# Storing results from GpSimd's queue in a two-layer convolution kernel, with rows of scales sent through DRAM

## The chip, the cores and the metric

The kernel runs on one core of one Trainium2 chip. A core has five engines that run side by side: TensorE (PE in the profile, with PEld for its weight loads), VectorE (DVE), ScalarE (ACT), GpSimd (POOL) and SyncE (SP). Any of SP, ACT and POOL can issue DMAs, and each has a queue of its own that works strictly in order: what waits at its head holds up all that stands behind it. The metric is the device time of one execution in microseconds (us), taken as the median of several runs.

## The reference

The input x is an activation of 16 images, 1024 channels, 32 x 32 pixels, in float32. Two residual blocks follow each other.

```python
# layer 0: a bottleneck with 3x3 self-attention in place of the 3x3 convolution
h = relu(bn(conv1x1(x, w_conv1)))                 # 1024 -> 256 channels
q, k = relu(bn(conv1x1(h, wq))), relu(bn(conv1x1(h, wk)))
v = bn(conv1x1(h, wv))
attn = softmax over the 9 taps of (q . (unfold3x3(k) + pos))     # 32 heads of 8 channels
h = relu(bn(sum over taps of unfold3x3(v) * attn))
x = relu(bn(conv1x1(h, w_conv3)) + x)             # 256 -> 1024 channels
# layer 1: an ordinary bottleneck
out = relu(bn(conv1x1(x, w1)))                    # 1024 -> 256
out = relu(bn(conv3x3(out, w2)))                  # 256 -> 256
x = relu(bn(conv1x1(out, w3)) + x)                # 256 -> 1024
```

The batch norm of layer 1 is built from mean, variance, gamma and beta. In the last products of both layers the scale of the norm is multiplied into the columns of the weights ahead of time; this needs the scale of each of the 1024 output channels as a row, the same in all 128 partitions.

## The kernel before

**Tiling.** Channels lie on the 128 partitions. An image has 8 chunks of 128 channels x 1024 pixels, 512 KB each. All products are float32 with 512 columns; one chunk of eight products takes PE 3.43 us. The stages of an image are written with a letter each:

- C (`first_conv`): 8 chunks of x are reduced to the 256 hidden channels (`reduce_part`, L360).
- Q and V (`project`, L446): q, k and v. They are written to DRAM and read back in another layout, by quarters of an image and heads. The reading back is called a relay here (`relay`, L534): q, k and the position terms together, and v.
- attention, on DVE alone (`logits` and `weighted`, L553 to L621): products of q with shifted k, sums over 8 channels, softmax (whose exp is L585 on ACT), and the weighted sum of shifted v. Its result a goes through DRAM back to the first layout.
- F (`fused`): for each of the 8 chunks the product of a with w3 on top of the residual, ReLU, a store of the result r to DRAM for later, and at once the reduction of that chunk with u1 for layer 1. The hidden result goes to `vh`, and DVE transforms it (`transform`, L668 to L679) for a Winograd form of the 3x3 convolution.
- W (`winograd_conv`, L737): the 3x3 convolution of four images together.
- U (`last_sum`): for each of the 8 chunks the product with u3 on top of the residual r, ReLU, and the store of the output.

**Expanding products.** F and U share the class `Expand`. `seed` (L384, ACT) copies a residual chunk, loaded from DRAM, into PSUM, two chunks ahead; `products` (L391, PE) adds to it; `result` applies ReLU with the bias (L410, ACT), in place in the chunk that held the residual, and issues the store of it (L411), on ACT's queue.

**Chunk buffers.** `xpool` has 8 buffers for chunks. `more_loads` issues the next loads in a fixed list (x for C, s for F, r for U, and the transformed V for W) whenever `credits` says that a buffer is free; the load (L336) goes out on POOL's queue, except for the first image's eight chunks of x, which go out on ACT's. In F and U `free(True)` gives a buffer back one chunk late, because the chunk's store has to land before the buffer is loaded again. Relays also go out on POOL's queue; weights, halves of attention's traffic and the scaled weights on SP's.

**Order.** The order of work on each engine is fixed when the program is built. The stages follow four lines of text; `Side` simulates DVE beside PE and decides between which chunks attention, transforms and weight preparation stand. Nothing is reordered on the chip.

**Semaphores of DMAs.** DMAs of SP and ACT take turns on eight completion semaphores, those of POOL on eight others. An issue waits until the DMA that had its semaphore before has landed.

**The start.** `at_first` loads eight chunks of x, then the taps of the 3x3 convolution (`load_taps`: six loads of 384 KB on ACT), then w3 and u3 for scaling (`load_scaled`: four of 512 KB on ACT), and four pieces of weights on SP. `winograd_weights` (L275 to L283, DVE and ACT) turns the taps into 36 Winograd weight planes. `scale_rows` (L225 to L238) makes the two rows of 1024 scales: DVE spreads the scales on diagonals (L229), PE multiplies them with a matrix of ones (L236), and ACT copies the result from PSUM (L238). `scale_weights` (L245) multiplies w3 and u3 with the rows on DVE.

Of the kernel before, what the change touches and what calls it, by code (L numbers as in the profile page):

```python
# [8 lines left out]
F32 = mybir.dt.float32  # L9
AF = mybir.ActivationFunctionType  # L10
ALU = mybir.AluOpType
AX = mybir.AxisListType

P = 128
B, C, H, W = 16, 1024, 32, 32
HW = H * W
WID = 256
NC = C // P
# [3 lines left out]
KK = 9  # L22
HEAD_DIM = 8
EPS = 1e-5
RELU = AF.Relu
CHUNKS = 8
NJ = 4
JROWS = H // NJ
JPIX = JROWS * W
PW = W + 2  # L30
HALO = (JROWS + 2) * PW
# [40 lines left out]
def sa_bottleneck_kernel(ctx: ExitStack, tc: tile.TileContext, x, w1t, wqkvt, w3t, u1t, u2t, u3t, params, out):  # L72
    nc = tc.nc
# [3 lines left out]
    const = ctx.enter_context(tc.tile_pool(name="const", bufs=1))  # L77
# [3 lines left out]
    apool = ctx.enter_context(tc.tile_pool(name="apool", bufs=1))  # L81
    ppool = ctx.enter_context(tc.tile_pool(name="ppool", bufs=2))
    zpool = ctx.enter_context(tc.tile_pool(name="zpool", bufs=3))
    psum = ctx.enter_context(tc.tile_pool(name="psum", bufs=4, space=bass.MemoryType.PSUM))
    dram = ctx.enter_context(tc.tile_pool(name="dram", bufs=1, space=bass.MemoryType.DRAM))
# [52 lines left out]
    def col(name, j, n=1):  # L138
        return par[:, _COL[name] + j : _COL[name] + j + n]
# [25 lines left out]
    for base, sign in ((0, 1), (HEAD_DIM - 1, -1)):  # L165
        nc.gpsimd.affine_select(
            out=members,
            in_=members,
            compare_op=ALU.is_ge,
            fill=0.0,  # L170
            base=base,
            pattern=[[-sign * HEAD_DIM, G]],
            channel_multiplier=sign,
# [7 lines left out]
    for n in range(NW):  # L181
# [12 lines left out]
        )  # L194


    ones = const.tile([P, P], F32, tag="ones", name="ones")
    nc.gpsimd.memset(ones, 1.0)
    eye = const.tile([P, P], F32, tag="eye", name="eye")
    nc.gpsimd.affine_select(  # L200
        out=eye, in_=ones, compare_op=ALU.is_equal, fill=0.0, base=0, pattern=[[-1, P]], channel_multiplier=1
    )

    kp = const.tile([P, NW, H + 2, PW], F32, tag="kp", name="kp")
    nc.gpsimd.memset(kp, 0.0)
    vh = const.tile([P, NW * VROWS, VW], F32, tag="vh", name="vh")

    scaled, scales = {}, []  # L210

# [12 lines left out]
    def scale_rows():  # L224

        for which, scale in enumerate((col("L0_conv_bn3_s", 0, NC), bn_inv[:, 2 * NW : 2 * NW + NC])):
            row = psum.tile([P, C], F32, tag="ps", name="row")
            diag = zpool.tile([P, HW], F32, tag="z", name="diag")
            nc.vector.tensor_tensor(  # L229
                diag.rearrange("p (o m) -> p o m", m=P),  # L230
                eye.unsqueeze(1).to_broadcast([P, NC, P]),
                scale.unsqueeze(2).to_broadcast([P, NC, P]),
                ALU.mult,
            )
            for half in range(2):
                nc.tensor.matmul(row[:, halves(half)], ones, diag[:, halves(half)], start=True, stop=True)  # L236
            scales.append(zpool.tile([P, HW], F32, tag="z", name="scales"))
            nc.scalar.activation(scales[which], row, AF.Identity)  # L238

    def scale_weights():  # L240

# [10 lines left out]

    taps = []

    def load_taps():
        n = 3 * WID

        for m, (tag, shape) in enumerate((("e", [P, KK, JPIX]), ("bnv", [P, HEAD_DIM, HALO]))):
            t = apool.tile(shape, F32, tag=tag, name="g").rearrange("p a b -> p (a b)")
            g = [t[:, i * n : (i + 1) * n] for i in range(3)]  # L260
            for i in range(3):
                nc.scalar.dma_start(g[i], u2t[m * P : (m + 1) * P, i * n : (i + 1) * n])
            taps.append(g)

    def winograd_weights():

# [46 lines left out]
    def halves(half):  # L313
        return slice(half * HALF, (half + 1) * HALF)


    loads, loaded, stored, credits, freed = [], {}, {}, [CHUNKS], []

    def more_loads():

        while credits[0] and loads:
            kind, b, c = loads[0]
            if kind == "V":
                if forms.get(b, 0) < NK:
                    return
                src = form_room(b)[c[0], c[1]].rearrange("p k j e -> p (k j e)")
            elif kind == "r":
                if (b, c) not in stored:
                    return
                src = stored[b, c]  # L330
            else:
                src = x[b, c * P : (c + 1) * P, :]
            t = xpool.tile([P, NK * 2 * PART], F32, tag="x", name=f"{kind}_{b}_{c}".translate(str.maketrans(" ,", "__", "()")))
            t = t if kind == "V" else t[:, :HW]

            (nc.scalar if kind == "x" and b == 0 else nc.gpsimd).dma_start(t, src)  # L336
            loaded[loads.pop(0)] = t
            credits[0] -= 1
# [34 lines left out]
    class Expand:  # L373
# [28 lines left out]
        def result(self, o, to):  # L402
            t = self.tiles.pop(o)
            ps, to_ = self.ahead.pop(o), t

            if self.kind == "s":
                ps, to_ = ps.rearrange("p (n j) -> p j n", j=4), t.rearrange("p (j n) -> p j n", j=4)
            else:
                ps, to_ = ps.rearrange("p (j n) -> p n j", j=4), t.rearrange("p (n j) -> p n j", j=4)
            nc.scalar.activation(to_, ps, RELU, bias=self.shift(o), scale=1.0)  # L410
            nc.scalar.dma_start(to, t)  # L411
            return t

    sums = {}
# [242 lines left out]
    def form_room(b):  # L657
        b -= b % NK
        if b not in form_rooms:
            form_rooms[b] = dram.tile([NI, 3, P, NK, 2, PART], F32, tag=f"v{b}", name="v")  # L660
        return form_rooms[b]
# [269 lines left out]
    for text in (  # L931
        "P0 P1 P2 P3 F0 P4 F1 P5 P6 F2 P7 F3 C8 Q8 W0 V8 C9 U0 Q9 V9 U1 U2 U3",
        "F4 F5 P10 F6 F7 C11 Q11 W4 V11 C12 U4 Q12 V12 U5 U6 U7",
        "F8 F9 P13 F10 F11 C14 Q14 W8 V14 C15 U8 Q15 V15 U9",
        "F12 F13 F14 U10:0123 F15 U10:4567 U11:0123 W12 U11:4567 U12 U13 U14 U15",
    ):
        for word in text.split():
            b, _, of = word[1:].partition(":")
            for letter in "CQV" if word[0] == "P" else word[0]:
                kind = {"C": "conv1", "Q": "qk", "V": "v", "F": "fused", "W": "wino", "U": "u3"}[letter]  # L940
                stages.append((kind, int(b), [int(o) for o in of] or range(NC)))
# [185 lines left out]
    made = []  # L1127

    def at_first():
        more_loads()  # L1130
        load_taps()
        load_scaled()
        for _ in range(4):
            more_weights()
        side.first(winograd_weights(), 24.0, 0.0)
        side.first(scale_weights(), 24.0, 0.0)
        scale_rows()
        hooks["conv1", 2, 0] = clear_hidden

    at_first()  # L1140
    for at in range(len(stages)):
        run(at)
# [40 lines left out]
```

## Time and profile before

| | before |
|---|---|
| time, median of 3 runs | 2469.91 us (2467.1 to 2471.02) |
| span of the profiled execution | 2473.1 us |
| PE busy | 2403.9 us, 97% |
| DVE busy | 2079.4 us, 84% |
| ACT busy | 933.5 us, 38% |
| POOL busy | 276.0 us, 11% |
| HBM traffic | 286 GB/s over the span |
| stores of r and of the output | 128 + 128, 512 KB each |
| loads of x, s and r from POOL | 120 + 128 + 128, 512 KB each |

The page gives the busy time of each engine, the chain of work that ended last, the costliest groups of instructions and the DMA issues. In a name such as `ps<-a,w` the tile written stands ahead of the arrow and the tiles read behind it. A name such as ACTq or SPq means the engine's sequencer, which issues DMAs; such an issue isn't counted as busy. The list of waits says for whom an engine stood idle: total, times, longest. A timeline line gives start, length, engine, line of the kernel, operation, tiles and, in brackets, the idle time before it and what ended it. L numbers are lines of the kernel before.

### The profile page before, as it was taken

The numbers are of one execution on the slowest core, as the hardware profiler recorded it, in microseconds if no ns is written. First come the engines' busy times: TensorE is split into PE (matmuls) and PEld (weight loads), VectorE is DVE, ScalarE is ACT, GpSimd is POOL, SyncE is SP. The second block draws the span as 40 slices with busy tenths as digits, with TensorE's granted clock in tenths as the row PEclk, the third lists the DMA queues.
The fourth block names the chain that finished last, engine by engine and source line by source line (L and its number), as shares of the span: only waits on it lengthen the run. The fifth ranks groups of instructions, "written<-read, shape, count | busy, mean of one in ns | idle before, by whom it ended". The sixth has DMA issues, their size and how long they took to land.

```text
span 2473.1 us, 18299 instructions
## 1 busy us (share of the span) xinstructions
PE 2403.9 (97%) x6152; PEld 1158.0 (47%) x6152; DVE 2079.4 (84%) x1633; ACT 933.5 (38%) x875; POOL 276.0 (11%) x523
## 2 busy tenths in 40 slices
PE   8999999999999999999989998999999989989999
PEld 3444444443475444444475443444466434434844
DVE  5899999998989999999789988899989989964700
ACT  4324142324123574243113573334122453344276
POOL 1110100010011111001011011001011010000111
PEclk9999999999999999999999999999999999989999
DMA  9969696978597998796598997688798887788887
GB/s 359 354 235 306 233 299 205 308 252 278 198 349 261 328 361 317 247 301 253 192 367 275 301 356 272 242 293 293 239 355 275 280 321 259 272 289 283 316 285 259
DMA packets 326060, 708.88 MB, mean 287 GB/s; under 512 B 20560, under 2 KB 199760, under 8 KB 317264
## 3 DMA queue, kind: packets, MB, share of 16 engines
q0 software_dynamic: 73728, 307.00, 35.5%
q1 hardware_dynamic: 203424, 249.39, 31.3%
q10 hardware_dynamic: 48816, 151.33, 15.7%
q8 instruction: 49, 0.80, 0.1%
q14 instruction: 43, 0.35, 0.0%
HBM read 432.62 MB, written 275.02 MB: 286 GB/s over the span
## 4 chain that ended last, share of the span: by engine, by line
PE 77%; DVE 10%; DMA 9%; ACT 2%; issue 1%; SPq 0%; ACTq 0%; DVEq 0%
PE ps L360 31%; PE ps L391 25%; PE ps L446 11%; PE ps L737 8%; DVE acc L604 3%; DVE acc L617 3%; DMA a<-a 2%; DMA U<-uw 2%; DMA q<-q 1%; DMA bnk<-kp 1%; DMA a<-acc 1%; DVE form L668 1%; PE ps L484 1%; DVE v L668 1%; DMA u<-in_u1t_dram 1%
## 5 line engine op out<-in xcount | busy, mean ns | idle before, releaser
L391 PE MATMUL ps<-a,w 128*128 128x512 f32 x1024 | 465.2, 600 | 14.6 <-ACT a L643 9.4
L360 PE MATMUL ps<-s,u 128*128 128x512 f32 x1024 | 462.8, 597 | 12.6 <-ACT s L410 12.5
L391 PE MATMUL ps<-y,u 128*128 128x512 f32 x1024 | 442.0, 593 | 1.9 <-ACT ps L384 1.9
L360 PE MATMUL ps<-x,w 128*128 128x512 f32 x1024 | 442.1, 592 | 0.0
L553 DVE TENSOR_TENSOR prod<-qc,bnk 128x2048 f32<-128x2048 f32 x144 | 324.0, 2287 | 14.3 <-DMA a<-acc 12.6
L604 DVE TENSOR_TENSOR acc<-e,bnv 128x2048 f32<-128x2048 f32 x144 | 327.5, 2283 | 3.6
L391 PEld LDWEIGHTS ps<-a,w 128*128 128x128 f32 x1024 | 196.6, 193 | 266.0 <-issue 227.4
L360 PEld LDWEIGHTS ps<-s,u 128*128 128x128 f32 x1024 | 195.5, 191 | 261.3 <-issue 235.2
L391 PEld LDWEIGHTS ps<-y,u 128*128 128x128 f32 x1024 | 194.2, 190 | 247.9 <-issue 226.6
L360 PEld LDWEIGHTS ps<-x,w 128*128 128x128 f32 x1024 | 194.6, 190 | 244.9 <-issue 244.2
L410 ACT ACTIVATE s<-ps,par 128x1024 f32<-128x1024 f32 x128 | 142.5, 1113 | 416.7 <-PE ps L391 414.9
L617 DVE TENSOR_TENSOR acc<-acc 128x2048 f32<-128x2048 f32 x128 | 293.4, 2292 | 4.4
L446 PE MATMUL ps<-h,wqk 128*128 128x512 f32 x512 | 225.8, 595 | 5.7 <-ACT h L989 5.7
L410 ACT ACTIVATE r<-ps,bn_sh 128x1024 f32<-128x1024 f32 x128 | 141.8, 1108 | 80.4 <-PE ps L391 78.4
L558 DVE TENSOR_TENSOR prod<-prod 128x2048 f32<-128x2048 f32 (+1 forms) x80 | 166.2, 2077 | 2.3
L446 PEld LDWEIGHTS ps<-h,wqk 128*128 128x128 f32 x512 | 96.2, 190 | 132.7 <-issue 110.0
L384 ACT ACTIVATE ps<-s 128x1024 f32<-128x1024 f32 x128 | 131.3, 1026 | 66.0 <-ACT s L410 42.3
L384 ACT ACTIVATE ps<-r 128x1024 f32<-128x1024 f32 x128 | 130.9, 1024 | 62.3 <-ACT r L410 34.9
L989 ACT ACTIVATE h<-ps,par 128x1024 f32<-128x1024 f32 x32 | 38.5, 1205 | 282.8 <-PE ps L360 282.8
L336 POOL DMA_DIRECT2D s<-in_x_dram x128 | 67.8, 529 | 647.0 <-PE ps L360 357.3
L336 POOL DMA_DIRECT2D x<-in_x_dram x120 | 63.6, 531 | 630.8 <-PE ps L360 387.7
L458 ACT ACTIVATE kp<-ps,par 128x1024 f32<-128x1024 f32 x64 | 77.3, 1208 | 141.8 <-PE ps L446 120.4
(312 smaller groups left out, 2125.4 us busy)
## 6 DMA issues: line engine op xcount, KB each, us to landing
s<-in_x_dram POOLq DMA_DIRECT2D x128, 512.0 KB, 6.3
r<-s ACTq DMA_DIRECT2D x128, 512.0 KB, 4.4
r<-r POOLq DMA_DIRECT2D x128, 512.0 KB, 6.0
out_dram<-r ACTq DMA_DIRECT2D x128, 512.0 KB, 5.5
x<-in_x_dram POOLq DMA_DIRECT2D x120, 512.0 KB, 4.4
v<-v SPq DMA_DIRECT2D x96, 408.0 KB, 5.4
U<-uw SPq DMA_DIRECT2D x72, 512.0 KB, 7.6
bnk<-kp SPq DMA_DIRECT2D x32, 680.0 KB, 8.4
```

Of the source, the lines that this page charges most:

```text
L336: (nc.scalar if kind == "x" and b == 0 else nc.gpsimd).dma_start(t, src)
L360: nc.tensor.matmul(ps[n][:, halves(half)], wt[:, c % (NC // 2), n * P : (n + 1) * P], src[:, halves(half)], start=(c == 0), stop=(c == NC ...
L384: nc.scalar.activation(ps, t, AF.Identity)
L391: nc.tensor.matmul(self.ahead[o][:, halves(half)], pieces[key][:, n, o % (NC // 2) * P :][:, :P], self.src[:, n, halves(half)], start=Fals ...
L410: nc.scalar.activation(to_, ps, RELU, bias=self.shift(o), scale=1.0)
L446: nc.tensor.matmul(ps[:, halves(half)], pieces[key][:, m, at : at + P], h[:, m, halves(half)], start=(m == 0), stop=(m == NW - 1),)
L458: nc.scalar.activation(dst, src, func, bias=col(f"L0_conv_{name}_b", n), scale=col(f"L0_conv_{name}_s", n),)
L553: nc.vector.tensor_tensor(by_row(t[:, two]), by_row(qc), kc[:, :, i : i + JROWS, j : j + W], ALU.mult)
L558: nc.vector.tensor_add(u[:, :, 0:4], u[:, :, 0:4], u[:, :, 4:8])
L604: nc.vector.tensor_tensor(by_row(dst), rows(e[:, k, :]).unsqueeze(1).to_broadcast([P, HEAD_DIM, JROWS, W]), vc[:, :, i : i + JROWS, j : j ...
L617: nc.vector.tensor_add(acc, acc, t)
L737: nc.tensor.matmul(acc[i][:, at, :, n, :], pieces[key][:, m, at, n * P : (n + 1) * P], v[:, at, :, m * (TILES + TR) :][:, :, :TILES], star ...
```

## The change

Four edits, in one step:

- **Stores.** `result` issues the store of a finished chunk on POOL's queue instead of ACT's. ACT then only computes there; POOL's queue holds loads, relays and stores in one order.
- **Rows of scales.** `scale_rows` no longer uses DVE, PE and ACT. The scales, which lie one per partition and chunk, are written to DRAM as one row of 1024 (in pieces of 4 bytes), and the row is read back into all 128 partitions. Both go on SP's queue. The matrix of ones and the identity are no longer made.
- **Taps.** The first image's loads are issued as four chunks of x, half of the taps, three chunks, the other half, the last chunk, so that the taps come earlier.
- **Order of U11.** The chunks of U11 are split 5 and 3 around W12 instead of 4 and 4, which shifts one chunk ahead of the Winograd stage.

```diff
--- before.py
+++ after.py
@@ -194,18 +194,11 @@
         )
 
 
-    ones = const.tile([P, P], F32, tag="ones", name="ones")
-    nc.gpsimd.memset(ones, 1.0)
-    eye = const.tile([P, P], F32, tag="eye", name="eye")
-    nc.gpsimd.affine_select(
-        out=eye, in_=ones, compare_op=ALU.is_equal, fill=0.0, base=0, pattern=[[-1, P]], channel_multiplier=1
-    )
-
-
 
     kp = const.tile([P, NW, H + 2, PW], F32, tag="kp", name="kp")
     nc.gpsimd.memset(kp, 0.0)
     vh = const.tile([P, NW * VROWS, VW], F32, tag="vh", name="vh")
+
 
     scaled, scales = {}, []
 
@@ -224,18 +217,11 @@
     def scale_rows():
 
         for which, scale in enumerate((col("L0_conv_bn3_s", 0, NC), bn_inv[:, 2 * NW : 2 * NW + NC])):
-            row = psum.tile([P, C], F32, tag="ps", name="row")
-            diag = zpool.tile([P, HW], F32, tag="z", name="diag")
-            nc.vector.tensor_tensor(
-                diag.rearrange("p (o m) -> p o m", m=P),
-                eye.unsqueeze(1).to_broadcast([P, NC, P]),
-                scale.unsqueeze(2).to_broadcast([P, NC, P]),
-                ALU.mult,
-            )
-            for half in range(2):
-                nc.tensor.matmul(row[:, halves(half)], ones, diag[:, halves(half)], start=True, stop=True)
-            scales.append(zpool.tile([P, HW], F32, tag="z", name="scales"))
-            nc.scalar.activation(scales[which], row, AF.Identity)
+            row = dram.tile([NC, P], F32, tag=f"row{which}", name="row")
+            nc.sync.dma_start(row.rearrange("o p -> p o"), scale)
+            t = zpool.tile([P, HW], F32, tag="z", name="scales")
+            nc.sync.dma_start(t, AP(row.tensor, row.offset, [[0, P], [1, C]]))
+            scales.append(t)
 
     def scale_weights():
 
@@ -252,15 +238,15 @@
 
     taps = []
 
-    def load_taps():
+    def load_taps(m):
         n = 3 * WID
 
-        for m, (tag, shape) in enumerate((("e", [P, KK, JPIX]), ("bnv", [P, HEAD_DIM, HALO]))):
-            t = apool.tile(shape, F32, tag=tag, name="g").rearrange("p a b -> p (a b)")
-            g = [t[:, i * n : (i + 1) * n] for i in range(3)]
-            for i in range(3):
-                nc.scalar.dma_start(g[i], u2t[m * P : (m + 1) * P, i * n : (i + 1) * n])
-            taps.append(g)
+        tag, shape = (("e", [P, KK, JPIX]), ("bnv", [P, HEAD_DIM, HALO]))[m]
+        t = apool.tile(shape, F32, tag=tag, name="g").rearrange("p a b -> p (a b)")
+        g = [t[:, i * n : (i + 1) * n] for i in range(3)]
+        for i in range(3):
+            nc.scalar.dma_start(g[i], u2t[m * P : (m + 1) * P, i * n : (i + 1) * n])
+        taps.append(g)
 
     def winograd_weights():
 
@@ -408,7 +394,7 @@
             else:
                 ps, to_ = ps.rearrange("p (j n) -> p n j", j=4), t.rearrange("p (n j) -> p n j", j=4)
             nc.scalar.activation(to_, ps, RELU, bias=self.shift(o), scale=1.0)
-            nc.scalar.dma_start(to, t)
+            nc.gpsimd.dma_start(to, t)
             return t
 
     sums = {}
@@ -932,7 +918,7 @@
         "P0 P1 P2 P3 F0 P4 F1 P5 P6 F2 P7 F3 C8 Q8 W0 V8 C9 U0 Q9 V9 U1 U2 U3",
         "F4 F5 P10 F6 F7 C11 Q11 W4 V11 C12 U4 Q12 V12 U5 U6 U7",
         "F8 F9 P13 F10 F11 C14 Q14 W8 V14 C15 U8 Q15 V15 U9",
-        "F12 F13 F14 U10:0123 F15 U10:4567 U11:0123 W12 U11:4567 U12 U13 U14 U15",
+        "F12 F13 F14 U10:0123 F15 U10:4567 U11:01234 W12 U11:567 U12 U13 U14 U15",
     ):
         for word in text.split():
             b, _, of = word[1:].partition(":")
@@ -1127,8 +1113,14 @@
     made = []
 
     def at_first():
+        credits[0] = 4
         more_loads()
-        load_taps()
+        load_taps(0)
+        credits[0] = 3
+        more_loads()
+        load_taps(1)
+        credits[0] = CHUNKS - 7
+        more_loads()
         load_scaled()
         for _ in range(4):
             more_weights()
```

## The prediction

> **What bounds the kernel now.** I read the page's busy shares and chain first, then what TensorE (PE) waited for, then the chain and ScalarE's (ACT's) timeline around its longest avoidable wait, last the DMA by stretch.
>
> ```profile
> PE 2403.9 (97%) x6152; PEld 1158.0 (47%) x6152; DVE 2079.4 (84%) x1633; ACT 933.5 (38%) x875; POOL 276.0 (11%) x523
> ...
> PE 77%; DVE 10%; DMA 9%; ACT 2%; issue 1%; SPq 0%; ACTq 0%; DVEq 0%
> ```
>
> PE works 2404 of 2473 us, so all that any change of queues can win is 69 us. VectorE (DVE) at 84% runs close beside it. Who held PE up:
>
> ```profile
> PE ps L360 <- ACT s L410: 12.5, 4, 7.7
> PE ps L737 <- issue: 10.5, 2, 8.0
> PE ps L391 <- ACT a L643: 9.4, 2, 4.8
> PE row L236 <- DVE diag L229: 8.0, 1, 8.0
> PE ps L391 <- ACT ps L384: 7.1, 5, 5.0
> ```
>
> Columns: total us, times, longest. The L410 and L384 rows (ReLU and seed) are ACT being late, the L643 row is image 15's attention arriving late, L236 is the start. The longest, 7.7 us at 1504.83, in ACT's timeline:
>
> ```profile
> 1492.02 1.11 ACT L410 ACTIVATE s<-ps,par 128x1024 f32<-128x1024 f32 x1 [2.32 <-PE ps L391]
> 1502.33 0.33 ACTq L411 DMA_DIRECT2D r<-s  x1
> 1502.71 1.03 ACT L384 ACTIVATE ps<-s 128x1024 f32<-128x1024 f32 x1 [9.58 <-DMA u<-in_u1t_dram]
> ```
>
> The ReLU ends at 1493.13, its store is issued only at 1502.33, and ACT stands still for 9.2 us. The chain there says for what:
>
> ```profile
> 1487.22 15.04 DMA u<-in_u1t_dram
> 1502.26 0.02 issue
> 1502.28 0.02 ACTq L411
> ```
>
> A store of s has no use for weights u. In the built program SP's and ACT's DMAs take turns on eight completion semaphores, and an issue waits until the semaphore's last DMA has landed. Five ACT stores wait over 1.6 us so: 5.9 before 940.51, 9.2 before 1502.33, 4.9 before 1977.60, 4.4 before 1999.35, 1.7 before 2100.14. PE shows two: 7.7 us at 1504.83, and 1.1 at 1983.85 with 5.0 at 2002.83.
>
> Last, the transfers: the issue lines (KB, us to landing), and two stretches of result chunks (columns: length; busy us of PE, PEld, DVE, ACT, POOL; clock; DMA share; GB/s):
>
> ```profile
> r<-s ACTq DMA_DIRECT2D x128, 512.0 KB, 4.4
> r<-r POOLq DMA_DIRECT2D x128, 512.0 KB, 6.0
> out_dram<-r ACTq DMA_DIRECT2D x128, 512.0 KB, 5.5
> ...
> 838.00:932.00 94.00, 93.84 (x219) 41.33 (x218) 89.06 (x53) 65.78 (x62) 14.16 (x27) 1.00 1.00 361
> ...
> 2344.00:2473.00 129.00, 124.16 (x291) 54.87 (x289) 10.22 (x16) 83.27 (x78) 15.35 (x29) 1.00 0.78 266
> ```
>
> The stages of u3 are where DMA is tight: one load and one store of 512 KB per 3.43 us, beside attention's traffic. Pairing each load's landing with the seed reading it, the residual is ready 0 to 6 us ahead in 858-925, 0 to 9 in 1420-1480 and 4 to 9 in the last 100 us, against 12 us or more in the stages of w3.
>
> **What the Trainium skill says.** "DMA: Bandwidth & Descriptors", section "Anatomy of one DMA": DMA engines do not wait on semaphores; the issuing sequencer waits before dispatch. The trace agrees: ACT's 9.2 us. Same page, "Issuing engines are not separate DMA queues": queues share 16 engines, so another queue saves only issue time (ACT's 0.33 us against GpSimd's (POOL's) 0.53 here). Section "Queues, rings and completion order": engines go round the queues packet by packet, each queue in order; so a store moved to POOL's queue lands behind the loads and relays issued before it. No view of before shows that case. "TensorE: Matmul & The Clock Gate", "What's actually happening": PE starts at half clock for about 3.4 us of work; here the first ones (L236) stood 0.86 us apart up to 12.45, then 0.43.
>
> **Part by part.**
>
> *Stores on POOL, ACT's side.* 256 issues of 0.33 us leave ACT (85 us, mostly beside idle time: ACT is 38% busy), and with them the semaphore waits. PE's stall at 1504.83 goes: 7.7 us plus about 0.7 at half clock after it, 8.4. At 1979-2003 5.0 + 1.1 and some 1.3 around them: 7. Do they reach the end? DVE waits for ACT's exp 16.5 us before 1552.26 (2.2 is the exp itself), for PE 7.0 before 1825.65, and 11.1 before 2001.89; so DVE moves up with PE. PE's waits for image 15's attention (4.8 at 2184, 4.6 at 2191) follow from DVE, so they move too. Upper bound 15.4; lower 8 if DVE keeps only the first. I take 15.
>
> *Stores on POOL, the queue's side.* POOL pays 256 x 0.53 = 136 us of issue on top of 276: not a bound. The cost is order. Built, the queue in a u3 stage runs: store k, load into the buffer of k-1, store k+1, load into that of k. The load waits for store k-1 to land, and store k+1 stands behind it. With landing time L two chunks then take at least L + 2 x 0.53 us; PE takes 6.87, so L up to 5.8 is free. In the last stretch stores land in 3.2 to 5 us: free. In 849-932 they took 4.3 to 7.7, mostly 6.5 to 7: 7 gives 8.1, or 0.6 us per chunk. Six images' u3, 48 chunks, lie in 838-932 and 1403-1490: none to 30 us, before slack of 3 to 6 us in each stretch. Fewer stores in flight also land sooner, which argues for the low part. Add the relays: q, k and positions (2.9 MB) go out on POOL at 787, 890, 1445; in 1448-1451 even ACT's stores took 9 us, and stores behind the relay may take 4 more. And the load of r at 829.04 now comes after a store issued at 849.94 while its seed starts at 852.80: about 3 us. Part of this hides: PE waits 8.0 us for DVE's transforms at 1249.33 anyway. I take 8 lost, from 0 to 30.
>
> In w3 stages the loads come some 4.1 us later (after the next ReLU, not just the last product), hidden by 12 us of slack. Relays are delayed by up to 30 us (579.30 to behind a store of 608.86), but q lands 87 us before its use at 675.6; the other delayed q and k relays, by up to 10 us, have 30 us or more. Nothing.
>
> *Rows of scales.* Off: DVE 2 x 1.22, PE 5.91, ACT 1.94 us. On, all on SP: twice a 4 KB store in 4-byte pieces, then a 512 KB load that waits for it. No row shows 4-byte data; a row store is at least the 2.3 us of the quickest load at the start (w, issued 0.81, landed 3.14) and, I estimate, at most the 8.7 of an x load behind a full queue; I take 4. The scales are first read at 80.58 (L245), so they are hidden themselves. But ACT's loads now take semaphores in turn with them: x7's issue waits for the second scales. That chain is x0's landing at 10.9 (its semaphore), row 4, then wv's landing at 18.0 (another), scales 8.7, so x7 goes out at 27 and lands at 32 (5 us). PE can begin when x0 has landed, 10.88, and now pays the half clock itself (some 2.2 us): as good as a start at 13.1 against 13.77, and x7 is due at 13.1 + 7 x 3.43 = 37.1. Hidden with 5 us to spare. Gain 0.7, from -3 (rows at 8.7 each) to 2.
>
> *Taps between chunks.* DVE waits 18.1 us for them before 27.23. The first three may land at 19 now. But ACT, which makes the second operand (L273, at 27.47 before), must first issue x7 and the w3/u3 loads behind it, at 27-28. No gain, from -2 to 2.
>
> *U11 split 5:3.* W12 starts 2.5 us late for the transforms' V and waits 1.9 for U; a chunk of 3.43 us moved ahead of W12 fills that. The stored buffer it holds delays V loads that have 6 us or more (landed 2296.7, used 2303.0). Gain 3, from 0 to 3.4.
>
> *End.* The last store is issued 0.2 us later and may land 0.3 later: -0.5.
>
> Sum: 15 + 0.7 + 0 + 3 - 8 - 0.5 = 10.2 us. 2469.9 - 10.2 = **2460**.
>
> **Rivals.** (1) *The whole gain stays*: with fewer DMAs taking SP's semaphores in turn and fewer stores in flight, nothing is lost in u3: 2469.9 - 18.2 = 2452. For it: PE was full at DMA 100% in 838-932. Against: 0 to 6 us of slack there. (2) *Eaten up*: the queue costs 18 instead of 8, and does it where DVE waits for ACT's exp (885.27 by 1.2 us, 1440.54 by 4.9), so that DVE slips as well: 2470. For it: those waits. Against: PE's 8.0 us to spare at 1249. (3) *Slower*: POOL's queue is the bound of u3 stages: 30 us of throttle and 12 of relays (4 each) against 12 of slack and 18 of gain: 2470 + 12 = 2482. For it: POOL's loads of r already wait 249 us for out stores. Against: landing time falls when fewer are in flight.
>
> **Numbers.** Forecast 0.48, rival 1 0.19, rival 2 0.13, rival 3 0.20. The low end, 2444, is rival 1 with DVE's waits for transfers before it (12.6 us at 1198.57, 5.2 at 411.53) shortened by 8 too. The high end, 2484, is rival 3 with the start 2 us worse. Faster by over 0.2% (under 2465): 0.66; within: 0.14; slower: 0.20.
>
> **What would show it.** Right: ACT has no idle time ended by a DMA that isn't its own data, and PE no 7.7 us at 1504; PE's first product comes at about 11 us; in u3 stages POOL's stores wait behind loads, and seeds (L384) wait for loads of r by some us near 852 and 1450; the gap before W12 is under 2 us. Wrong: seeds wait in the last 100 us, where landing time must stay under 5.8; PE waits for x7 in the first 40 us; DVE's waits for exp don't shrink with PE's stalls, so that the 15 us stay with PE; or relays reach DVE late.

## The result and the profile after

The changed kernel takes 2476.94 us (median of 4 runs, 2476.71 to 2478.05), the kernel before in the same session 2469.61 us. The ratio is 1.0032, with a 95% interval of 1.0014 to 1.0049: slower by 0.3%, where the prediction said 2460. A second measurement on another chip gave 1.0029 (1.0019 to 1.0040). The experiments below ran on chips on which the kernel before takes 2462 to 2465 us, so they are compared by ratio; 0.001 is about 2.5 us. A ratio is worked out over all runs and can differ by some 0.001 from the quotient of two medians. The profiled runs lie closer together than the medians: the one of before took 2475.2 us, the one of the changed kernel 2476.75.

First the busy times and the chain on the page of the changed kernel (L numbers are now its own: the seed L384 is L370, the products L391 are L377, the ReLU L410 is L396, the store L411 is L397, the products of C and of r with u1, L360, are L346; later, the lines of an experiment have the numbers of its own kernel).

```profile
PE 2399.6 (97%) x6144; PEld 1153.9 (47%) x6144; DVE 2076.7 (84%) x1631; ACT 919.0 (37%) x873; POOL 411.0 (17%) x777
...
PE 76%; DMA 12%; issue 5%; DVE 3%; ACT 1%; POOL 1%; ACTq 0%; SPq 0%; POOLq 0%; DVEq 0%
```

PE works as long as before; POOL has its 135 us of store issues, as predicted. The chain has changed hands: DMA was 9% and is 12%, and DVE fell from 10% to 3%. Next, the list of what PE waited for (total us, times, longest):

```profile
PE ps L346 <- DMA x<-in_x_dram: 24.1, 5, 9.3
PE ps L377 <- ACT ps L370: 12.1, 9, 3.6
PE ps L432 <- ACT h L975: 9.0, 13, 3.7
PE ps L723 <- issue: 6.3, 1, 6.3
...
PE ps L346 <- ACT s L396: 1.0, 1, 1.0
```

The last row answers to the 12.5 us of `ACT s L410` at the head of the list before: the waits of ACT's stores are gone, as predicted. The first row is new, 24.1 us for chunks of x. All of it lies in the first 54 us: 9.3 until PE's first product at 9.26 (before, the diagonals had 8.0 in that place), and 14.8 between the chunks after it. The wait for seeds grew from 7.1 to 12.1.

Where does the 24.1 come from? The chain of the first 80 us, cut to the pieces with the two rows (start, length, what):

```profile
5.57 14.10 DMA row<-par
19.68 0.34 SPq L223
...
20.12 21.22 DMA row<-bn_inv
41.36 0.35 ACTq L248
```

Two stores of 4 KB take 14.1 and 21.2 us from issue to landing. Part of that is SP's queue: the first stands behind the load of wv, which lands at 15.57, the second behind the first load of scales, which lands at 29.25. From there on they take 4.1 and 12.1 us more. A tap load on ACT goes out in the very moment in which the second row has landed, though it needs nothing of it: in the built program it has the next turn on that store's semaphore. x7 waits in the same way for the second load of scales: issued at 47.38 and landed at 53.42, against a forecast of 27 and 32. Image 0's hidden result comes from ACT at 61.7 us instead of 39.7. What it waits for last is the taps: PE is done with x7's products at 59.2, but ACT, which works in order, is still at the taps, the first of which it could begin only at 49.84.

Busy times by stretch say what else was slow. First the kernel before, then the changed one (length; busy us of PE, PEld, DVE, ACT, POOL; granted clock; DMA share; GB/s):

```profile
6.00:20.00 14.00, 11.98 (x23) 5.30 (x24) 2.96 (x8) 0.00 (x0) 0.69 (x1) 1.00 1.01 379
20.00:42.00 22.00, 22.00 (x52) 9.50 (x50) 13.02 (x25) 10.13 (x19) 3.48 (x7) 1.00 1.04 397
```

```profile
6.00:20.00 14.00, 10.74 (x21) 4.82 (x22) 0.37 (x4) 0.00 (x0) 1.21 (x2) 1.00 0.89 210
20.00:42.00 22.00, 14.39 (x28) 5.71 (x27) 0.96 (x1) 0.00 (x0) 1.58 (x3) 0.84 0.93 266
```

The DMA engines are still busy 89 and 93% of the time, but they move 210 and 266 GB/s instead of 379 and 397. The page counts 22672 packets under 512 bytes where it counted 20560: the 2112 more are mostly the 2048 pieces of 4 bytes. The trace's records of single packets show that the pieces themselves are short, 0.01 us each. It is the packets of the other transfers that become long. Those of 2 KB and more (mostly 4 KB) take 0.15 to 0.16 us on average from 26 to 32 us; from 12 to 20 us, while the first row is written, they take 0.31 to 0.95, and from 32 to 38 us, while the second is, 0.26 to 1.21.

Later the lost 22 us come back, though not steadily. The changed kernel is behind by 23.0 us at the first fused stage (240.1 against 217.1 us), 17.5 at the first Winograd stage, 27.0 at F6 (1114.5 against 1087.5), 14.7 at F9, 2.3 at F13, and 0.5 at PE's end. That is the stores' gain, less what they cost. What they cost is seen in GpSimd's timeline, behind a relay (start, length, operation, and in brackets the idle time before it and what ended it):

```profile
916.66 0.53 POOL L520 DMA_DIRECT2D qc<-q  x1
...
918.22 0.54 POOL L397 DMA_DIRECT2D out_dram<-r  x1
920.22 0.53 POOL L322 DMA_DIRECT2D r<-r  x1 [1.46 <-DMA out_dram<-r]
920.74 0.54 POOL L397 DMA_DIRECT2D out_dram<-r  x1
930.97 0.53 POOL L322 DMA_DIRECT2D r<-r  x1 [9.69 <-DMA out_dram<-r]
...
937.53 0.53 POOL L322 DMA_DIRECT2D r<-r  x1 [3.01 <-DMA out_dram<-r]
```

The store issued at 918.22 lands only behind the relays of 916.66 to 917.70, and at the head of the queue the next load but one waits 9.7 us for it, with every later store and load behind. ACT's seed, at 932.03, has waited 8.2 us for its chunk of r. From then on load and store go in lockstep: each load waits until the last store but one before it has landed, and the next store stands behind that load. This takes 3.5 to 4.2 us per chunk where PE takes 3.43. The same happens behind the relay of 1466.72. The issue lines (KB, us to landing) show it as longer landings, 5.1 for r and 6.5 for the output, against 4.4 and 5.5 on ACT's queue:

```profile
r<-s POOLq DMA_DIRECT2D x128, 512.0 KB, 5.1
r<-r POOLq DMA_DIRECT2D x128, 512.0 KB, 5.8
out_dram<-r POOLq DMA_DIRECT2D x128, 512.0 KB, 6.5
```

And at W12 the loads of the transformed V stand behind the output stores of U11:

```profile
2274.86 0.53 POOL L397 DMA_DIRECT2D out_dram<-r  x1 [2.95 <-ACT r L396]
2275.55 0.53 POOL L322 DMA_DIRECT2D V__0_8020<-v  x1 [0.16 <-issue]
```

The first v's that it needs had landed by 2270.52. The load goes out 5 us later, after the fourth store of U11, lands at 2283.03, and PE stands 6.3 us, against 2.5 before.

### The profile page after: what moved, and what is told of

Its sections match the earlier page's. It is cut to its first block, busy times and chain, and to the rows that moved or that the text cites. A ratio compares the mean times of both kernels' runs of the same rounds, so it can differ in the third digit from the quotient of the medians.

```text
span 2474.9 us, 18390 instructions
## 1 busy us (share of the span) xinstructions
PE 2399.6 (97%) x6144; PEld 1153.9 (47%) x6144; DVE 2076.7 (84%) x1631; ACT 919.0 (37%) x873; POOL 411.0 (17%) x777
## 2 busy tenths in 40 slices
DMA packets 328429, 709.94 MB, mean 287 GB/s; under 512 B 22672, under 2 KB 201872, under 8 KB 319632
## 4 chain that ended last, share of the span: by engine, by line
PE 76%; DMA 12%; issue 5%; DVE 3%; ACT 1%; POOL 1%; ACTq 0%; SPq 0%; POOLq 0%; DVEq 0%
PE ps L346 33%; PE ps L377 23%; PE ps L432 12%; DMA out_dram<-r 7%; PE ps L723 7%; DMA q<-q 1%; PE ps L470 1%; DMA row<-bn_inv 1%; POOL r L322 1%; DVE acc L590 1%; DMA U<-uw 1%; DVE acc L603 1%; ACT h L975 1%; DMA s<-in_x_dram 1%; DMA row<-par 1%
## 5 line engine op out<-in xcount | busy, mean ns | idle before, releaser
L377 PE MATMUL ps<-a,w 128*128 128x512 f32 x1024 | 463.2, 597 | 10.0 <-ACT ps L370 5.2
L346 PE MATMUL ps<-x,w 128*128 128x512 f32 x1024 | 449.5, 599 | 24.1 <-DMA x<-in_x_dram 24.1
L346 PE MATMUL ps<-s,u 128*128 128x512 f32 x1024 | 458.2, 592 | 1.0 <-ACT s L396 1.0
L377 PE MATMUL ps<-y,u 128*128 128x512 f32 x1024 | 444.9, 595 | 7.1 <-ACT ps L370 6.9
L346 PEld LDWEIGHTS ps<-x,w 128*128 128x128 f32 x1024 | 196.7, 193 | 273.7 <-issue 251.1
L377 PEld LDWEIGHTS ps<-a,w 128*128 128x128 f32 x1024 | 194.9, 191 | 260.7 <-issue 239.6
L396 ACT ACTIVATE s<-ps,par 128x1024 f32<-128x1024 f32 x128 | 142.5, 1113 | 463.3 <-PE ps L377 390.7
L377 PEld LDWEIGHTS ps<-y,u 128*128 128x128 f32 x1024 | 194.4, 191 | 255.7 <-issue 236.9
L346 PEld LDWEIGHTS ps<-s,u 128*128 128x128 f32 x1024 | 194.3, 190 | 246.7 <-issue 237.5
L397 POOL DMA_DIRECT2D r<-s x128 | 68.2, 533 | 732.4 <-ACT s L396 715.7
L396 ACT ACTIVATE r<-ps,bn_sh 128x1024 f32<-128x1024 f32 x128 | 141.8, 1109 | 105.6 <-PE ps L377 100.7
L370 ACT ACTIVATE ps<-r 128x1024 f32<-128x1024 f32 x128 | 130.4, 1021 | 58.5 <-DMA r<-r 45.5
L370 ACT ACTIVATE ps<-s 128x1024 f32<-128x1024 f32 x128 | 131.1, 1024 | 22.5 <-DMA s<-in_x_dram 18.8
L746 ACT ACTIVATE z<-ps 128x1024 f32<-128x1024 f32 x48 | 49.0, 1024 | 183.4 <-PE ps L723 127.8
```

What stands on the lines that cost most here:

```text
L346: nc.tensor.matmul(ps[n][:, halves(half)], wt[:, c % (NC // 2), n * P : (n + 1) * P], src[:, halves(half)], start=(c == 0), stop=(c == NC ...
L370: nc.scalar.activation(ps, t, AF.Identity)
L377: nc.tensor.matmul(self.ahead[o][:, halves(half)], pieces[key][:, n, o % (NC // 2) * P :][:, :P], self.src[:, n, halves(half)], start=Fals ...
L397: nc.gpsimd.dma_start(to, t)
```

## The experiments

Theory after the result: the way of the scales through DRAM lost the 22 us, and the stores would have won. The rival: delays at the start are soaked up by later waits anyway, and the stores on GpSimd's queue lose.

| run | what it has | us | before | ratio, 95% interval |
|---|---|---|---|---|
| e1_rows_back | changed, rows on TensorE again | 2453.37 | 2465.13 | 0.9954 (0.9938 to 0.9970) |
| e2_only_rows | before + rows through DRAM | 2495.25 | 2465.13 | 1.0110 (1.0093 to 1.0128) |
| e3_only_stores | before + all stores on GpSimd | 2453.39 | 2465.13 | 0.9948 (0.9936 to 0.9960) |
| e4_only_taps | before + taps between chunks | 2466.85 | 2465.13 | 1.0009 (0.9998 to 1.0019) |
| e5_after_again | the changed kernel | 2470.65 | 2462.39 | 1.0029 (1.0019 to 1.0040) |
| e6_rows32 | changed, rows in 32-byte pieces | 2455.23 | 2462.39 | 0.9967 (0.9956 to 0.9978) |
| e7_rows32_hold2 | e6 + loads held back one store | 2445.44 | 2462.39 | 0.9925 (0.9911 to 0.9938) |
| e8_rows_on_pool | changed, row stores on GpSimd | 2464.50 | 2462.39 | 1.0012 (1.0002 to 1.0023) |
| e9_rows_back_hold2 | e1 + loads held back one store | 2436.82 | 2463.43 | 0.9888 (0.9866 to 0.9911) |
| e10_stores_u11 | e3 + split of U11 | 2448.65 | 2463.43 | 0.9937 (0.9914 to 0.9959) |
| e11_out_on_pool | before + output stores on GpSimd | 2468.41 | 2463.43 | 1.0020 (1.0008 to 1.0031) |
| e12_r_on_pool | before + stores of r on GpSimd | 2435.16 | 2463.43 | 0.9885 (0.9865 to 0.9905) |
| e13_only_u11 | before + split of U11 | 2462.31 | 2462.39 | 1.0002 (0.9991 to 1.0012) |
| e14_r_on_pool_u11 | e12 + split of U11 | 2434.44 | 2462.39 | 0.9891 (0.9876 to 0.9907) |

**The parts one by one.** In e1 the rows are made as before, and the rest of the change stays:

```diff
-            row = dram.tile([NC, P], F32, tag=f"row{which}", name="row")
-            nc.sync.dma_start(row.rearrange("o p -> p o"), scale)
-            t = zpool.tile([P, HW], F32, tag="z", name="scales")
-            nc.sync.dma_start(t, AP(row.tensor, row.offset, [[0, P], [1, C]]))
-            scales.append(t)
+            row = psum.tile([P, C], F32, tag="ps", name="row")
...
+            for half in range(2):
+                nc.tensor.matmul(row[:, halves(half)], ones, diag[:, halves(half)], start=True, stop=True)
+            scales.append(zpool.tile([P, HW], F32, tag="z", name="scales"))
+            nc.scalar.activation(scales[which], row, AF.Identity)
```

> The changed kernel with one part undone: the rows of scales are made on TensorE and ScalarE again; stores on GpSimd's queue, taps between the first chunks and the new split of U11 stay. Theory A (the way through DRAM lost the time: its two row stores of 14.1 and 21.2 us put the start 22 us behind, and nothing later gave that back): first products and h 0 at the times of the kernel before (within 3 us), and the whole some 20 us under the changed kernel, 2455 to 2459 us. Rival B (the delay of the start is soaked up by later waits on VectorE, and the stores on GpSimd's queue are what loses): the start comes back but the end moves by under 7 us, 2470 to 2476 us.

Measured: 0.9954. Image 0's hidden result is 0.4 us behind the first profile of before, and against the changed kernel (1.0032) the ratio is 0.9923, some 19 us. Theory A holds.

e2 is the kernel before with the lines marked minus above put in.

> The kernel before with one part alone: the rows of scales through DRAM. Theory A: row stores of 14 and 21 us again, stalls of TensorE near 32 and 53 us, +18 to +24 us at the end: 2488 to 2494 us. Rival B (soaked up later): under +8, 2470 to 2478 us. Rival C (the slow row needs the company of the taps and more loads around it, which this kernel does not have in that place): row stores under 10 us and +0 to +5 us.

Measured: 1.0110, 27 us, more than any theory said; the profiled run was the quickest, 20 us above the median of before. The rows alone take 14.1 and 24.7 us, and here the taps stand behind x7 in ACT's queue, so that image 0's hidden result comes at 65.4. Rival C fell: the rows are as slow without the early taps beside them.

e3 is the kernel before with one word changed:

```diff
-            nc.scalar.dma_start(to, t)
+            nc.gpsimd.dma_start(to, t)
```

> The kernel before with one part alone: results are stored by GpSimd's queue. Theory A (the stalls at 598, 1249, 1504 and 1977 to 2003 us go, some 8, 7, 8 and 6 us, and loads behind waiting stores lose 6 us each in the two u3 stages of r and 3 us in W0): 2456 to 2460 us. Rival B (what the lockstep of stores and loads takes equals what ScalarE wins): 2467 to 2472 us.

Measured: 0.9948, a gain of 12.8 us, near the upper end of what theory A gave. The rival of a net zero fell.

e4 has the new `load_taps(m)` and the order of `credits` of the diff, and nothing else.

> The kernel before with one part alone: the taps are loaded between the first chunks, with the credits of the changed kernel. Theory A: no row store slows the transfers, so nothing waits for the taps: 2467 to 2472 us. Rival: the order of loads itself puts chunk 7 behind the taps, a stall of 2 to 6 us of TensorE before 60 us that stays to the end: 2472 to 2476 us.

Measured: 1.0009, no difference that the interval shows. Chunk 7 comes in time: image 0's hidden result is at 39.4.

**What in the rows cost it: the size of the pieces or the turns?** e5 is the base for the next three.

> The changed kernel once more, as the base on this chip for the three kernels beside it. Every theory: slower than the kernel before by 0.2 to 0.6%, row stores of about 14 and 21 us again, first h of TensorE's chunks some 22 us behind.

The time came as expected. The rows took 16.1 and 14.3 us here, and the hidden result came at 58.1, 18 us late and not 22. e6 keeps queue, order and waits, and changes the pieces:

```diff
-            row = dram.tile([NC, P], F32, tag=f"row{which}", name="row")
-            nc.sync.dma_start(row.rearrange("o p -> p o"), scale)
+            row = dram.tile([P, NC], F32, tag=f"row{which}", name="row")
+            nc.sync.dma_start(row, scale)
...
-            scales.append(t)
+            scales.append(t.rearrange("q (p o) -> q o p", o=NC))
```

> The changed kernel, with the rows of scales stored in the order in which a partition holds them, 128 pieces of 32 bytes in place of 1024 of 4 bytes, and read back as before; VectorE reads the scales through a view with a step of 8 elements. The queues, waits and the order of issue stay. Theory A (the 4-byte pieces cost the time): row stores of 2 to 5 us each, no stall of TensorE over 3 us before 60 us, h 0 within 4 us of the kernel before, and the whole 0.3 to 0.7% under the kernel before. Rival B (the turns cost it: transfers of ScalarE's queue that wait for the scales issued on SyncE's, whatever the size of their pieces): the first x of image 0 and the taps still wait for the scales, h 0 stays 10 us or more behind, and the whole is within 0.3% of the kernel before. Rival C: the strided read slows VectorE's products by 2 us and more each, and h 0 or the first attention is late for that.

The chain at its start:

```profile
5.56 10.31 DMA row<-par
...
16.33 5.67 DMA row<-bn_inv
```

The whole gains 16 us over the changed kernel (0.9967 against 1.0029 to 1.0032), as theory A has it. Its row stores are longer than the 2 to 5 us that it gave, but by SP's queue alone: wv lands at 15.66 and the first row 0.2 us later, the first scales at 21.64 and the second row 0.4 us later. Of the 35 us in the changed kernel, then, some 19 are this queue and 16 (4.1 and 12.1) the small pieces. x7 goes out at 29.2 us, where the prediction's chain had 27. That the two are so near is in part luck: the chain had left out what stands ahead of the rows in SP's queue. The hidden result comes at 43.5, 4 us behind e4's; the turns cost no more than that here. Rival C is true in small: the four products with the view's step of 8 take 2.02 to 2.04 us each (L233) instead of 1.22 (L245 before), 3.2 us of DVE in all.

e8 leaves the pieces in the program and takes away the turns behind them: the same two 4-byte stores on GpSimd's queue, read back there in the stage of image 1.

```diff
-            nc.sync.dma_start(row.rearrange("o p -> p o"), scale)
+            nc.gpsimd.dma_start(row.rearrange("o p -> p o"), scale)
```

> The changed kernel with the same two 4-byte row stores at the same place of the program, but on GpSimd's queue, and the scales read back on that queue only in the stage of image 1. No transfer of ScalarE's or SyncE's then has to take its turn behind them. Theory A1 (the small pieces hold up whatever moves beside them): the transfers from 6 to 42 us still run at 60 to 75% of the kernel before, h 0 is 8 to 20 us behind, and the whole is 5 us and more above the kernel with rows of 32 bytes. Theory A2 (small pieces are only slow themselves, and the turns made the others wait for them): the throughput of the first 42 us stays within 10% of the kernel before, h 0 under 5 us behind, and the whole is within 4 us of the kernel with rows of 32 bytes.

Transfers and PE at its start (GB/s in 40 slices of the first 40 us; then PE's first work):

```profile
GB/s 0 28 274 214 291 76 306 331 345 96 97 101 99 121 96 97 96 254 351 168 126 355 412 412 406 414 401 417 393 426 411 394 415 402 405 410 401 405 395 395
```

```profile
15.51 30.36 PE L352 MATMUL ps<-x,w 128*128 128x512 f32 x64 [15.51 <-DMA x<-in_x_dram]
```

For 8 us, from 9 to 17, while both rows are under way (they land at 15.5 and 19.3), everything together moves 96 to 121 GB/s; from 22 us on it is some 400. PE's first chunk arrives at 15.5 us instead of 9.3. So small pieces hold up what moves beside them, as theory A1 says, also where nothing has its turn behind them. Its figures were too large: from 6 to 42 us 79% of the kernel before's transfers are moved, and the hidden result is 6.4 us behind, between the two theories. The whole, 1.0012, does not measure the start alone: reading the scales at 90 us made DVE wait 13.5 us for them (L237), which is this kernel's own fault. Nor is e8 the changed kernel without its turns: its page counts only 96 packets under 512 bytes more than before's, so that on GpSimd's queue the pieces don't show as packets of their own.

How the 22 us of the start divide between the turns and the slowed transfers stays open. In the two stretches above (379 to 210 GB/s over 14 us, 397 to 266 over 22 us) transfers worth 6.2 + 7.3 = 13.5 us were not moved. Some of them were slowed, as the long packets show, and some were not yet issued; these runs don't tell how many.

**What in the stores cost and won.** e7 adds one thing to e6: in `free(True)`, two buffers in place of one are held back.

```diff
-            credits[0] += len(freed) - 1
-            del freed[1:]
+            credits[0] += max(0, len(freed) - 2)
+            del freed[2:]
```

> The kernel with rows in pieces of 32 bytes, with one thing more: in the u3 stages a load is released only with the second store before it, so that GpSimd's queue does not stand at a load that waits for the store just issued. Theory A (loads and stores in lockstep on one queue cost 4 to 7 us at each of the two places near 930 and 1480 us): the gaps of GpSimd behind its relays stay, but the lockstep after them goes, and the whole is 4 to 12 us under the kernel without it. Rival B (the stores behind the relay are late anyway, and one buffer less in flight costs what the lockstep did): within 3 us of it, or slower.

Measured: 0.9925 against 0.9967, 10 us. PE's waits for seeds, first in e6, then in e7:

```profile
PE ps L377 <- ACT ps L370: 12.1, 6, 4.7
```

```profile
PE ps L377 <- ACT ps L370: 1.3, 2, 1.0
```

With the edit the output stores also land sooner, in 4.9 us instead of 6.5. The lockstep is real. e9 has this edit on top of e1.

> The two things that the runs so far point to, together: the changed kernel with the rows of scales made on TensorE again, and with loads in the u3 stages released only by the second store before them. Theory A (the start and the lockstep are separate losses, and their cures add): the ratio of the first, 0.9954, and what the held-back buffer gave in pieces of 32 bytes, 0.9925 / 0.9967 = 0.9958, give 0.991, so 2440 to 2445 us where the kernel before takes 2463 to 2465. Rival B (the later start of the kernel with 32-byte rows was soaked up, so that its cure gives nothing): 0.9925 again.

Measured: 0.9888, 16 us under e1 and 27 us under the kernel before: somewhat more than expected, though the interval just reaches theory A's 0.991. In its timeline of GpSimd the head of the queue still waits behind the relay, but shorter, and the chunks behind it catch up at 2.5 to 3.2 us each, under PE's 3.43:

```profile
899.44 0.53 POOL L338 DMA_DIRECT2D r<-r  x1 [5.05 <-DMA out_dram<-r]
...
904.43 0.53 POOL L338 DMA_DIRECT2D r<-r  x1 [1.29 <-DMA out_dram<-r]
```

e11 and e12 part the two kinds of stores: the output's alone (`self.kind == "r"`), and those of r alone (`"s"`).

```diff
-            nc.scalar.dma_start(to, t)
+            (nc.gpsimd if self.kind == "r" else nc.scalar).dma_start(to, t)
```

> The kernel before, with the stores of the last results alone (stage u3, the output) moved to GpSimd's queue; stores of r stay on ScalarE's. Theory A (the gain of ScalarE's side lies in both kinds of stage, the lockstep of loads and stores comes where loads of r wait for stores): about half of the gain of all stores, TensorE's stalls at 1977 to 2003 us gone, those at 598 and 1504 us still there, 0.996 to 0.9985. Rival B (these stores are the ones that cost on GpSimd's queue, since loads share it): 1.000 or above, and the kernel that moves the other kind takes 0.993 or less.

> The kernel before, with the stores of r alone (the fused stages) moved to GpSimd's queue; the output's stores stay on ScalarE's. Theory A: the stalls at 598 and 1504 us gone, those at 1977 to 2003 us still there, and no lockstep after the relays near 917 and 1467 us, since the queue's stores there are the output's: 0.994 to 0.998. Rival B: the fused stages gain nothing without the others, 0.999 to 1.001.

Measured: 1.0020 and 0.9885. Rival B of e11 is right: output stores on GpSimd's queue win nothing and cost 5 us alone, and beside the stores of r they cost 0.9948 against 0.9885, 15 us. The stores of r won all there was, 28 us, twice the most that theory A gave them. In e11 PE's waits for seeds (11.0 us) and for DVE's transforms (16.7) are each 6 us above those of e4, a kernel no different from before in time. PE's waits in e4, then in e12:

```profile
PE ps L360 <- ACT s L410: 16.2, 4, 10.6
PE ps L737 <- issue: 10.5, 2, 6.5
...
PE ps L391 <- ACT ps L384: 4.9, 6, 1.5
```

```profile
PE ps L737 <- issue: 4.8, 2, 3.2
...
PE ps L391 <- ACT ps L384: 3.5, 4, 1.6
...
PE ps L360 <- ACT s L410: 0.6, 1, 0.6
```

The wait for stores of r (`ACT s`) fell from 16.2 to 0.6 us, and that for DVE's transforms (`issue` at L737) from 10.5 to 4.8. One thing stays open: in e11, too, the wait for `ACT s` is only 6.3 us, though its stores of r are still on ACT. Fewer DMAs then take turns on SP's and ACT's semaphores, and each has another turn; no run here separates that from the kind of store that moved.

**The split of U11.** e10 is e3 with the new order of stages, e13 the kernel before with it, e14 the stores of r with it:

```diff
-        "F12 F13 F14 U10:0123 F15 U10:4567 U11:0123 W12 U11:4567 U12 U13 U14 U15",
+        "F12 F13 F14 U10:0123 F15 U10:4567 U11:01234 W12 U11:567 U12 U13 U14 U15",
```

> The kernel before with two parts: results on GpSimd's queue and the later start of W12 within U11. Theory A (the split still gives the 3 us of the prediction; what stood against it at W12 comes from the stores alone): the stall of TensorE ahead of W12's products is 6 to 7 us, against 9.5 with the stores alone, and the whole 1 to 4 us under the stores alone, a ratio of 0.9933 to 0.9945. Rival B (the split moves the stall and nothing else): 0.9948, as with the stores alone, or above.

> The kernel before with one part alone: W12 starts one chunk of U11 later. Theory A (the term of the prediction, 3 us, is right as long as no store stands ahead of W12's loads): the stall ahead of W12's products falls from about 4 us to 1 or less, and the whole is 2 to 4 us under the kernel before, 0.9984 to 0.9992. Rival B (the loads of V move with the split, so that the stall stays): stall of 3 us and more, 0.9995 to 1.0008.

> The kernel before with the stores of r alone on GpSimd's queue and the later start of W12. Theory A (as above): the stall of 3.4 us ahead of W12's products, which the kernel with the stores of r alone has, goes, and the whole is 2 to 4 us under it: 0.987 to 0.9877, some 2432 us where the kernel before takes 2463. Rival B: 0.988 to 0.989, no different from the stores of r alone.

Measured: e10 0.9937, whose interval holds e3's 0.9948; PE's wait ahead of W12 is 6.6 us against 9.3, as theory A said. e13 is 1.0002 and e14 0.9891 against e12's 0.9885: no gain. In e13 the wait ahead of W12's first product is gone, and another stands 10 us later:

```profile
2276.10 5.08 PE L737 MATMUL ps<-V__1_8034,U 128*128 128x256 f32 x16 [3.33 <-DMA U<-uw]
```

With an extra chunk ahead of it W12 starts at much the same time as in e4 (2265.6 against 2267.2 us), its third group of products then waits for weights U, and starts as late as in e4 (2276.1 against 2275.8). Rival B's outcome, though by another wait than it named.

e9, e12 and e14 are the quickest, all near 0.989; their intervals don't part them.

## Why the prediction was wrong, step by step

**Rows of scales: the step that failed.** The prediction gave a row store "at most the 8.7 of an x load behind a full queue; I take 4", and the whole edit a gain of 0.7, from -3 to 2. Measured: 14.1 and 21.2 us, and a loss of 19 us (e1 against the changed kernel) or 27 (e2). The mechanism of the turns was put right: x7's issue does wait for the second scales. The upper bound was not, for two reasons. It left out the order on SP's queue, where the rows stand behind wv and the first scales: for that alone the first row took 10.3 us in e6. And it took the price of a transfer by its bytes, from a load of 512 KB in long pieces: the small pieces added 4.1 and 12.1 us. The Trainium skill would have warned of it. Its page "DMA: Bandwidth & Descriptors", section "Rules for kernel authors", says that a last dimension that isn't contiguous becomes one descriptor for each element, and section "Specifications" puts line rate at 512 bytes and more. The packet count and the GB/s above agree. Neither section prices 1024 such pieces, but they forbid a bound taken from a transfer with long ones. And what is queued or moves beside the pieces pays too: "hidden with 5 us to spare" needed x7 by 37.1, and it landed at 53.4. The forecast followed x7 only; the tap load that waited for the second row's semaphore, until 41.36, made the hidden result later still.

**Stores, ACT's side: the mechanism right, the sizes wrong.** Of the 15 us predicted, 8.4 were for the stall at 1504, behind a store of r, and 7 for those near 2000, behind output stores. The stores of r alone won 28 (e12), the output's alone lost 5 (e11), and the waits near 2000 are still 2.9 us in e12. Against e4, the wait for `ACT s` falls by 15.6 us over all fused stages (the forecast left out the one at 598, 4.3 us in e4), and those for transforms and weights U by 8.4; among the latter is the wait for transforms at 1249, 6.5 to 1.6, which the forecast took as given. Waits for seeds and attention fall by 2.4, those for z and q grow by 4. PE's own busy time is 7.2 us shorter on top (2390.4 against 2397.6), since fewer products follow a stall: the first four after the stall at 1504 took 3.4 us in e4, other fours 2.0. That makes 29.6 us between two profiles whose spans differ by 29.7. "DVE moves up with PE" held.

**Stores, the queue's side: right, and too small, and at other places.** 8 us predicted, from 0 to 30; measured 15 (e12 against e3) and 16 (e9 against e1). The throttle by landing times over 5.8 us without relays wasn't seen: in that stretch of the changed kernel, from 864 to 929 us, PE runs without a wait. What costs is "stores behind the relay", put at 4 us each: seeds waited 8.2 us near 930, 5.0 near 1480, and the lockstep kept the queue from catching up. The other place is W12, where V's loads stand behind output stores: PE waits 9.3 us there in e3, 3.2 in e12, and the forecast had no term for it. The late load of r near 852 cost nothing that shows. The sum of both sides, 7 predicted, was 12.8 in e3: both terms were about half of what was measured, and that their difference came so near is luck.

**Taps: right.** 0 predicted, 1.0009 measured.

**U11: wrong in size.** 3 predicted, nothing measured (e13, e14). The 2.5 us of wait for V and 1.9 for U were not two parts of one delay that a chunk could fill: with V's wait filled, U is still late. In the changed kernel, with output stores ahead of V's loads, PE waits 6.3 us there, split and all.

**End.** -0.5 predicted. PE ends 0.5 us later than before and the kernel 1.8, so 1.3 us of it are the last stores' landing.

With the terms as measured the sum has the right sign: 12.8 for the stores less 19 to 27 for the rows is 6 to 14 us slower, where 7 to 8 are measured. So the rival named slower had the right side and the wrong cause: it laid the loss on GpSimd's queue, which in the end still let the stores win.

## What to carry to other kernels

Price a small DMA by its pieces: two stores of 4 KB took 35 us in pieces of 4 bytes here and 16 in pieces of 32, and the small pieces slowed what moved beside them. Count also what stands ahead of it on its queue. Before moving stores to a queue that also holds loads, ask of each kind of store whether a load behind it waits for that very store and what large transfer stands ahead; here one kind won 28 us, and the other lost 5 alone and 15 beside the first. An edit that fills one wait wins nothing while the next operand is late as well.

## What the runs showed of the hardware

- A store of 1024 pieces of 4 bytes took 14.1 and 21.2 us among other loads (14.1 and 24.7 in e2, 16.1 and 14.3 in e5; 11.8 and 13.8 from GpSimd's queue in e8). In the changed kernel 4.1 and 12.1 us of this came after the landing of the transfer ahead of it; with 128 pieces of 32 bytes it was 0.2 and 0.4.
- A piece of 4 bytes took 0.01 us as a packet, but packets of 2 KB and more beside such pieces took 0.26 to 1.21 us on average, against 0.15 to 0.16 in a stretch between. All transfers together moved 96 to 121 GB/s for 8 us in e8, and about 400 from 22 us on.
- VectorE's product of 128x1024 float32 took 1.22 us with its second operand in order and 2.02 with a step of 8 elements.
- Waits for a completion semaphore's turn held ACT for up to 9.2 us at an issue, and taking half of the stores away from it was worth 1.15% of a kernel in which ACT is busy 38% of the time.
- A load that waits at the head of GpSimd's queue for the last store but one before it turned one late landing (9.7 us behind 2.9 MB of relays) into a lockstep of 3.5 to 4.2 us per chunk, over six chunks.
